# Graph attention followed by a graph convolution: p v by 26 products per 4-by-4 blocks of p instead of 28, with the block sums on GpSimd

## The chip, the cores and the metric

One core of a Trainium2 chip runs the whole program; the other cores are idle. The metric is device time in microseconds (us). Everything is in float32. The engines are called as in the profile: PE (TensorE, matmuls; PEld are its weight loads), DVE (VectorE), ACT (ScalarE), POOL (GpSimd) and SP (SyncE, which here only issues DMAs).

## The reference

```python
# x: 4096 x 512, adj: 4096 x 4096 (symmetric pattern, about 1 % of entries set)
q, k, v = x @ Wq.T + bq, x @ Wk.T + bk, x @ Wv.T + bv
a = q @ k.T / sqrt(512) + adj + adj
x = layernorm(x + softmax(a) @ v)
h = relu(adj @ (x @ W1) + b1)          # W1: 512 x 128
x = layernorm(x + adj @ (h @ W2) + b2)
```

Layer 0 has two large products, the scores q k^T and p v (p is the softmax's numerator). Layer 1 has two products with adj, of 128 columns each.

## The kernel before, in words

**Products of blocks.** Each large product is made of 2-by-2 blocks with seven block products in place of eight (Winograd's form). Sums of blocks of the left and of the right operand are made ahead on DVE and POOL or read from DRAM, and each product's PSUM result is added to the output quarters by DVE. ORDER (1, 2, 6, 7, 5, 4, 3) is the order of the seven; products 1, 6, 5, 3 collect in one PSUM bank and 2, 7, 4 in another, so that sums over products come from the accumulation in PSUM.

**Groups, units and gaps.** Scores and p are held transposed: keys on partitions, queries along columns. The 4096 queries are eight groups g of 512 columns. A group's scores take 16 units (two units for each 512 keys, d = 0 to 7), and a unit has seven gaps. In the main loop a gap does this in order: the hooks put there (`at`, `run`); a pair of score matmuls (`qk`, L423, 128x256, K of 256); if the pair is the second of its product, the read of its PSUM bank (`qk_read`, L436, one DVE add of 128x512 into S, where adj already lies); then the p reads that were due before the gap began; then items from a list `todo`, as many as a budget in us allows. A matmul item of p v counts 0.43. The schedule is by hand: each engine carries out its instructions in the order in which the program gives them out.

**What stands in the lists.** During group 0's scores the list holds the products for u = M x (`u_fast`, L243) and v = x Wv (`v_fast`, L342, one call for each 512 rows) for all rows, and the sums of v's blocks (`sum_v`, L371: four of 128x512 on POOL for each 512 rows; `store_v`, `store_sums`). During the scores of group g + 1 it holds group g's p v, from unit 2 on, and around it the rows of the group before (`row_items`, L663: division by the sum, residual, layer norm, `add_b2`, and the projection by W1, `project` and `project2`). The last group's p v has no scores beside it. Then come the products with adj (L979, `strassen`) and the output rows.

**From scores to p.** `new_max` (L445, DVE, 128x512) keeps a running maximum; when the group is done it is turned and spread; `shift` (L469, DVE, 128x512) subtracts it, and `exps` (L473, ACT, 128x1024) takes the exponential in place, two key tiles at a time. PREP says in which unit and gap each is done.

**p v before.** `px_items` (L536) goes through the 16 pairs of key tiles in five blocks of 2, 2, 4, 4, 4 pairs (BLOCKS). In each block it takes the seven products in ORDER; one product has two row halves r and accumulates over the block's pairs, one matmul (L553, 128x257 or 128x256, K of 128) for each pair and half: 16 x 7 x 2 = 224 matmuls a group, 1792 in all. The 257th column is a column of ones beside v, which gives the softmax's denominator. The left operand's sums are made in place in S, pair by pair: `px_t2` (L494, L495) on POOL, `px_t34` (L501) and `px_t1` (L506) on DVE in between the products. The right operands, blocks of v and their sums, are loaded by SP, one DMA of 256 or 512 KB for each product of a block (`load_x`, L485), three ahead. `px_read` (L524) adds a PSUM result to the output tile OT, 560 reads in all.

**What else lies in the way of these.** `add_b2` (L638) makes x1 + b2 on POOL (L641) in a tile `xb` of the ring of eight `sa` tiles (the pool `sap`), and POOL issues its store (L643); SP fills the other places of that ring with score operands (`load_s`, L307 and L312). The pool `adjp` has 12 slots of 1 MB for S, for v's tiles and, later, for chunks of adj, given out by the framework's pool in turn. The PSUM tag "o" has four banks, also in turn; x and y hold the scores.

Of the kernel before, what the change touches and what calls it, by code (L numbers as in the profile page):

```python
# [20 lines left out]
CW = 1024  # L21


@with_exitstack
def tile_graph_attention_then_gcn(
# [87 lines left out]
    BLOCKS = ((0, 2), (2, 4), (4, 8), (8, 12), (12, 16))  # L113
    vs_d = {a: dram.tile([P, 7, b - a, HW], F32, name=f"vs_d{a}") for a, b in BLOCKS}
# [11 lines left out]
    xnp = att.enter_context(tc.tile_pool(name="xnp", bufs=2, side="right"))  # L126
    form = ExitStack()
    mp = form.enter_context(tc.tile_pool(name="mp", bufs=1, side="right"))
    m_t = mp.tile([P, ND, D], F32, name="m_t")
    g_t = mp.tile([P, D], F32, name="g_t")  # L130
    ms_t = mp.tile([P, 2, 2, HW], F32, name="ms_t")
    xtp = form.enter_context(tc.tile_pool(name="xtp", bufs=2, side="right"))
    uop = form.enter_context(tc.tile_pool(name="uop", bufs=1, side="right"))

    def bank(tag, name, bufs=1):
        return psum.tile([P, W], F32, tag=tag, name=name, bufs=bufs)
# [59 lines left out]
    def u_fast(b):  # L196
# [41 lines left out]
        def one(k, j):  # L238
            def go():
                if j == 0 and k in (1, 2, 7):  # L240
                    X["X" if k == 1 else "Y"] = bank("o", f"psu{b}_{k}", 4)
# [72 lines left out]
    def x_rows(q):  # L314

        w = xnp.tile([P, 2, D], F32, tag="xn", name=f"w{q}", padded_shape=[P, 2, D + 4])
        nc.sync.dma_start(w, x[ts(q, 2 * P), :].rearrange("(r p) d -> p r d", p=P))
        T["x_rows", q] = lambda r: row_parts(2 * q + r, w[:, r])

    def v_fast(d):  # L320
# [3 lines left out]
        def read(k):  # L324
            ps = X["X" if k in (1, 6, 5, 3) else "Y"].rearrange("p (j o) -> p j o", j=2)
            t, o = QUARTER[k]
            to = VW[d][:, 2 * t + o]
            if k in (1, 6, 7, 3):
                nc.scalar.copy(to, ps)
            else:  # L330
                nc.vector.tensor_tensor(to, ps, to, ALU.add)
            if k == 4:
                store_v(d)

        def one(k, j):
            def go():
                if (k, j) == (1, 0):
                    VW[d] = v_room(d)
                if j == 0 and k in (1, 2, 7):
                    X["X" if k == 1 else "Y"] = bank("o", f"psv{d}_{k}", 4)  # L340
# [21 lines left out]
    def v_place(d):  # L362
        a = max(a for a, _ in BLOCKS if a <= 2 * d)
        return vs_d[a][:, :, 2 * d - a : 2 * d - a + 2, :]

    def store_v(d):
        to = v_place(d)
        nc.scalar.dma_start(to[:, 0], VW[d][:, 0])
        nc.scalar.dma_start(to[:, 1:3], VW[d][:, 2:4])

    def sum_v(d):  # L371
        a11, a21, a12, a22 = (VW[d][:, k] for k in range(4))
        tt = nc.gpsimd.tensor_tensor
        tt(a22, a21, a22, ALU.add)
        tt(a21, a21, a11, ALU.subtract)
        tt(a11, a22, a11, ALU.subtract)
        tt(a12, a12, a11, ALU.subtract)

    def store_sums(d):
        nc.gpsimd.dma_start(v_place(d)[:, 3:7], VW[d])  # L380


    def begin_scores(g, d):

        S[g, d] = adjp.tile([P, 2, 2, W], F32, tag="adj", name=f"s{g}_{d}")
# [85 lines left out]
    def exps(g, q):  # L471
        ck = pair(g, q)
        nc.scalar.activation(ck, ck, AF.Exp, scale=2.0)  # L473

    PHASES = [(g, a, b, k) for g in range(NG) for a, b in BLOCKS for k in ORDER]

    def load_x(n):
        g, a, b, k = PHASES[n]
        if n < 4:
            pool = xnp2 if n % 4 > 1 else xnp  # L480
            XN[n] = pool.tile([P, 4, HW + 1], F32, tag="xn", name=f"xn{n}")
            nc.gpsimd.memset(XN[n][:, :, HW:], 1.0)
        XN[n] = XN[n % 4]
        place = {1: 0, 2: 1, 4: 2, 6: 3, 7: 4, 3: 5, 5: 6}[k]
        nc.sync.dma_start(XN[n][:, : b - a, :HW], vs_d[a][:, place])  # L485

    def quarters(g, q):
        ck = pair(g, q)
        return ck[:, 0, :HW], ck[:, 0, HW:], ck[:, 1, :HW], ck[:, 1, HW:]

    def px_t2(g, q):

        b11, b12, _, b22 = quarters(g, q)
        nc.gpsimd.tensor_tensor(b12, b12, b11, ALU.subtract)  # L494
        nc.gpsimd.tensor_tensor(b12, b22, b12, ALU.subtract)  # L495

    def px_t34(g, q):

        b = pair(g, q)[:, :, :HW]
        t2 = pair(g, q)[:, 0, HW:].unsqueeze(1).to_broadcast([P, 2, HW])  # L500
        nc.vector.tensor_tensor(b, b, t2, ALU.subtract)  # L501

    def px_t1(g, q):

        _, t2, _, b22 = quarters(g, q)
        nc.vector.tensor_tensor(t2, b22, t2, ALU.subtract)  # L506
# [3 lines left out]
    def px_read(g, first, k, r):  # L510

        letter = "PX" if k in (1, 6, 5, 3) else "PY"
        ps = T[letter, r][:, : HW + 1]
        f, i = QUARTER[k]
        to = OT[g][:, 2 * i + r, f]

        def go():
            if first and k in (1, 6, 7, 3):
                if g == NG - 1:
                    nc.vector.tensor_copy(to, ps)  # L520
                else:
                    nc.scalar.copy(to, ps)
            else:
                nc.vector.tensor_tensor(to, ps, to, ALU.add)  # L524

        px_reads.append((letter, go))

    def read_px(letters=("PX", "PY")):
        for one in list(px_reads):
            if one[0] in letters:  # L530
                px_reads.remove(one)
                one[1]()
# [3 lines left out]
    def px_items(g):  # L536
        def one(n, r, q):
            _, a, b, k = PHASES[n]

            def go():  # L540
                letter = "PX" if k in (1, 6, 5, 3) else "PY"
                if q == a:
                    if r == 0:
                        if n + 3 < len(PHASES):
                            load_x(n + 3)
                        if k in (6, 5, 3, 4, 7):
                            read_px((letter,))
                        if k == 1 and a == 0:
                            OT[g] = rowp.tile([P, PER, 2, HW + 1], F32, tag="ot", name=f"ot{g}", bufs=2)
                    if k in (1, 2):  # L550
                        T[letter, r] = bank("o", f"p{n}_{r}", 4)
                cols = HW + (k != 6)
                nc.tensor.matmul(  # L553
                    T[letter, r][:, :cols],
                    quarters(g, q)[{1: 0, 2: 2, 6: 1, 7: 0, 5: 1, 4: 2, 3: 3}[k]][:, ts(r, P)],
                    XN[n][:, q - a, :cols],
                    start=k in (1, 2, 7) and q == a,
                    stop=q == b - 1,
                    skip_group_check=True,
                )  # L560
                if r == 1:
                    if k == 6:
                        px_t34(g, q)
                    if k == 7:
                        px_t1(g, q)
                if q == b - 1:
                    px_read(g, a == 0, k, r)
# [4 lines left out]
            one(n, *((m % 2, a + m // 2) if k in (6, 7) else (m // (b - a), a + m % (b - a))))  # L572
            for n, (g_, a, b, k) in enumerate(PHASES)
            if g_ == g
            for m in range(2 * (b - a))
# [87 lines left out]
    def row_items(g, between):  # L663
# [6 lines left out]
        def pro(r):  # L670
            return [item(0.44, project, g, r)]

        def pro2(r):
            return [item(0.9, project2, g, r)]
# [15 lines left out]
    with tc.tile_pool(name="wqk", bufs=1) as wp:  # L690
# [53 lines left out]
        for o in range(ND):  # L744
            turned(wq_t, wq_n, o, bank("o", f"psq{o}", 4))
# [5 lines left out]
        psm = [bank("o", f"psm{a}", 4) for a in range(ND)]  # L751
# [30 lines left out]
    SLOTS = 12  # L782

    adjp = ctx.enter_context(tc.tile_pool(name="adjp", bufs=SLOTS))
    v_ring = [adjp.tile([P, 4, 2, HW], F32, tag="adj", name=f"vw{n}") for n in range(3)]
    wv_t = adjp.tile([P, 2, 2, 2, HW], F32, tag="adj", name="wv_t")
    v_ring.append(t_sb[:, :16].rearrange("p (k j a) b -> p k j (a b)", k=4, j=2))

    def v_room(d):
        return v_ring[(0, 1, 2, 0, 1, 3, 2, 3)[d]]  # L790

    wv_t4 = accp.tile([P, 2, HW], F32, tag="lacc", name="wv_t4")
# [36 lines left out]
    for d in range(NG):  # L829
        if d:  # L830
            first += [(0.86, f) for f in u_fast(d)]
        late = [(0.86, f) for f in v_fast(d)]
        if d:
            late[4:4] = [(0, lambda d=d: sum_v(d - 1))]
            late[12:12] = [(0, lambda d=d: store_sums(d - 1))]
        first += late
    first += [
        (0.86, lambda: owing.pop()()), (0.86, lambda: sum_v(NG - 1)), (0, lambda: store_sums(NG - 1))
    ]
# [75 lines left out]
    def load_to(u):  # L915

        while len(CK) < min(2 * u + 2, len(loads)):
            j, tiles, i, cols = loads[len(CK)]
            ck = adjp.tile([P, tiles, cols], F32, tag="adj", name=f"ck{len(CK)}")
# [14 lines left out]

    def b_side(u):
# [7 lines left out]
        def t13(m):  # L943
            TT[m] = adjp.tile([P, 3, W], F32, tag="adj", name=f"tt{m}")
# [13 lines left out]
    def open_block(n):  # L958
        w = blocks[n][2]
        BK[n] = {  # L960
            k: bank(BANKS[k], f"b{n}_{k}", 4 if BANKS[k] == "o" else 1)[:, :w] for k in (1, 2)
        }

    def product(u, k):

        n, q0, pairs = UNITS[u]
        if k not in BK[n]:
            w = blocks[n][2]
            BK[n][k] = bank(BANKS[k], f"b{n}_{k}", 4 if BANKS[k] == "o" else 1)[:, :w]
# [17 lines left out]
    def strassen(n, beside, done=()):  # L987
# [51 lines left out]
    EARLY, MID, LATE = (1, 2, 4), (2, 4, 6), (3, 5, 6)  # L1039
    PREP = [  # L1040
        (1, (2, 3, 4)), (1, (4, 5, 6)), (2, LATE), (3, MID), (4, EARLY), (4, LATE), (5, EARLY), (5, LATE),
# [271 lines left out]
```

## Time and profile before

| | |
|---|---|
| median of three runs | 2307.99 us (2307.57 to 2308.24) |
| the profiled execution | 2308.46 us, of which the profile's span is 2306.7 |
| mean granted TensorE clock | 0.996 |
| instructions in the span | 28379 |
| group 1's first add_b2 tile to group 2's (L641) | 778.58 to 981.51 us |
| DMA traffic | 528 MB, 229 GB/s over the span; 203 to 207 GB/s in mid-kernel, 331 in the stretch from 1900 us |

Times in a profile line are us; in a group's line the columns are the form and count, then busy time and mean ns of one, then the idle time of the engine just before and what ended most of it. A PE record is a half of a matmul: one float32 matmul of the program leaves two MATMUL records and two weight loads, so the 1792 matmuls of p v are x3584 at L553. In a timeline line the columns are start, duration, engine, line, operation and form, and in brackets how long the engine was idle before and what ended it. In a line of windows the columns are the window, its length, then busy time and count for PE, PEld, DVE, ACT and POOL, the granted clock, the share of the DMA engines' time, and GB/s.

### The profile page before, as it was taken

To read this page: it belongs to the slowest core of one execution; us is meant where nothing else is said; L and a number is where in the kernel's file an instruction comes from. 1 tells how busy PE (TensorE), PEld (TensorE's weight loads), DVE (VectorE), ACT (ScalarE), POOL (GpSimd) and SP (SyncE) were. 2 spreads that over 40 slices of the span, in tenths; PEclk is the share of its full clock that TensorE was granted. 3 is DMA by queue.
4 is the path that set the end of the run, shared out by engine and by line. 5 is a ranking of instruction groups with operands and counts; after the bars stand their busy time and mean duration, and the time that the engine had idled before them with its cause. 6 is when DMAs were issued, how large, how long until landed. Compare 5 with 4: busy or idle time off the path is not lost.

```text
span 2306.7 us, 28379 instructions
## 1 busy us (share of the span) xinstructions
PE 2270.1 (98%) x10732; PEld 1769.0 (77%) x10732; DVE 1475.5 (64%) x2526; ACT 287.9 (12%) x409; POOL 534.2 (23%) x651
## 2 busy tenths in 40 slices
PE   9999999999999999999999999999998999999998
PEld 6888888888888888888888888888886743333455
DVE  5454556656656665665666567566656877888864
ACT  2111111002101100210120021002002100000012
POOL 2242341112211311231131123113113720101143
PEclk9999999999999999999999999999999999999999
DMA  5656676574665667466666756666546568999996
GB/s 184 210 214 213 220 265 217 184 258 160 219 223 190 211 192 251 157 216 222 200 191 203 254 164 210 218 211 196 193 155 219 173 250 329 333 349 375 356 377 196
DMA packets 324791, 528.27 MB, mean 229 GB/s; under 512 B 18416, under 2 KB 190960, under 8 KB 323504
## 3 DMA queue, kind: packets, MB, share of 16 engines
q1 hardware_dynamic: 272128, 404.81, 52.7%
q10 hardware_dynamic: 43408, 85.21, 10.5%
q0 software_dynamic: 9120, 36.44, 4.1%
q8 instruction: 86, 1.41, 0.2%
q14 instruction: 49, 0.40, 0.0%
HBM read 472.13 MB, written 52.69 MB: 228 GB/s over the span
## 4 chain that ended last, share of the span: by engine, by line
PE 89%; issue 5%; DVE 4%; POOL 1%; DMA 0%; ACT 0%; POOLq 0%; DVEq 0%; ACTq 0%
PE p L553 29%; PE X L423 18%; PE b L979 14%; PE Y L423 13%; PE psv L342 4%; PE psu L243 4%; PE acce L1258 2%; PE tps L658 1%; PE ops L1212 1%; DVE s L501 1%; PE x1ps L649 1%; DVE stats L623 1%; PE psm L754 1%; DVE s L469 0%; DVE s L436 0%
## 5 line engine op out<-in xcount | busy, mean ns | idle before, releaser
L553 PE MATMUL p<-xn,s 128*128 128x257 f32 (+1 forms) x3584 | 913.7, 381 | 14.4 <-DVE s L501 9.4
L553 PEld LDWEIGHTS p<-xn,s 128*128 128x128 f32 x3584 | 678.8, 191 | 120.0 <-DVE s L501 13.2
L423 PE MATMUL X<-ut,sa 128*128 128x256 f32 x1984 | 513.6, 381 | 3.8 <-DVE s L436 3.8
L423 PEld LDWEIGHTS X<-ut,sa 128*128 128x128 f32 x1984 | 369.3, 189 | 68.8 <-DVE s L436 20.3
L436 DVE TENSOR_TENSOR s<-X,s 128x512 f32<-128x512 f32 x256 | 176.8, 690 | 322.4 <-PE X L423 321.8
L423 PE MATMUL Y<-ut,sa 128*128 128x256 f32 x1408 | 360.6, 379 | 0.0
L494 POOL TENSOR_TENSOR s<-s 128x256 f32<-128x256 f32 x128 | 102.6, 802 | 881.1 <-ACT s L473 879.9
L436 DVE TENSOR_TENSOR s<-Y,s 128x512 f32<-128x512 f32 x192 | 132.6, 691 | 265.9 <-PE Y L423 265.7
L423 PEld LDWEIGHTS Y<-ut,sa 128*128 128x128 f32 x1408 | 265.7, 189 | 37.1 <-DVE s L436 0.2
L473 ACT ACTIVATE s<-s 128x1024 f32<-128x1024 f32 x128 | 135.3, 1057 | 833.9 <-DVE s L469 829.9
L524 DVE TENSOR_TENSOR ot<-p,ot 128x257 f32<-128x257 f32 x496 | 202.3, 418 | 36.7 <-PE p L553 36.1
L469 DVE TENSOR_TENSOR s<-s,mb 128x512 f32<-128x512 f32 x256 | 189.3, 741 | 7.4 <-ACT mb L399 7.4
L445 DVE TENSOR_TENSOR macc<-macc,s 128x512 f32<-128x512 f32 x240 | 183.7, 765 | 0.3
L946 DVE TENSOR_TENSOR tt<-ck 128x1024 f32<-128x1024 f32 x112 | 139.3, 1280 | 36.2 <-PE b L979 31.5
L979 PE MATMUL b<-tt,st 128*64 128x512 f32 (+1 forms) x768 | 159.1, 545 | 3.1 <-DVE tt L950 3.1
L979 PEld LDWEIGHTS b<-tt,st 128*64 128x64 f32 x768 | 55.1, 138 | 93.5 <-issue 79.5
L495 POOL TENSOR_TENSOR s<-s 128x256 f32<-128x256 f32 x128 | 105.8, 827 | 10.0
L979 PE MATMUL b<-ck,t_sb 128*64 128x512 f32 x384 | 96.7, 595 | 0.0
L501 DVE TENSOR_TENSOR s<-s 128x512 f32<-128x512 f32 x128 | 93.7, 746 | 0.0
L950 DVE TENSOR_TENSOR tt<-ck,tt 128x512 f32<-128x512 f32 x112 | 81.7, 765 | 0.0
L581 POOL TENSOR_TENSOR xr<-xr,bv_t 128x512 f32<-128x512 f32 x32 | 43.6, 1394 | 136.9 <-DMA xr<-in_x_dram 119.9
L954 DVE TENSOR_TENSOR ck<-ck,tt 128x512 f32<-128x512 f32 x112 | 73.7, 693 | 0.0
(175 smaller groups left out, 1750.2 us busy)
## 6 DMA issues: line engine op xcount, KB each, us to landing
ck<-in_adjT_dram SPq DMA_DIRECT2D x128, 1024.0 KB, 7.5
xn<-vs_d SPq DMA_DIRECT2D x168, 512.0 KB, 4.3
s<-in_adjT_dram ACTq DMA_DIRECT2D x64, 1024.0 KB, 7.1
sa<-s_d SPq DMA_DIRECT2D x224, 256.0 KB, 4.4
sa<-in_xT_dram SPq DMA_DIRECT2D x168, 256.0 KB, 4.7
xn<-vs_d SPq DMA_DIRECT2D x112, 256.0 KB, 2.9
ut<-u_d SPq DMA_DIRECT2D x49, 256.0 KB, 6.9
xt<-in_xT_dram SPq DMA_DIRECT2D x8, 1024.0 KB, 9.2
```

The costliest lines, as they stand in the source:

```text
L423: nc.tensor.matmul(T["X" if k in (1, 6, 5, 3) else "Y"][:, ts(j, HW)], SA[g, d, a][:, c, j, :], UT[g, b][:, c, :], start=k in (1, 2, 7) an ...
L436: nc.vector.tensor_tensor(ck, ps, ck, ALU.add)
L445: nc.vector.tensor_tensor(MACC[g], MACC[g], ck[:, h, :], ALU.max)
L469: nc.vector.tensor_tensor(ck, ck, MB[g], ALU.subtract)
L473: nc.scalar.activation(ck, ck, AF.Exp, scale=2.0)
L494: nc.gpsimd.tensor_tensor(b12, b12, b11, ALU.subtract)
L495: nc.gpsimd.tensor_tensor(b12, b22, b12, ALU.subtract)
L501: nc.vector.tensor_tensor(b, b, t2, ALU.subtract)
L524: nc.vector.tensor_tensor(to, ps, to, ALU.add)
L553: nc.tensor.matmul(T[letter, r][:, :cols], quarters(g, q)[{1: 0, 2: 2, 6: 1, 7: 0, 5: 1, 4: 2, 3: 3}[k]][:, ts(r, P)], XN[n][:, q - a, :cols],
L946: nc.vector.tensor_tensor(t[:, :2], v[:, :, 1], v[:, 0], ALU.subtract)
L979: nc.tensor.matmul(BK[n][k][ts(half, HH)], lhs, right(u, i, half, b), start=q == 0, stop=q == NP - 1,)
```

## The change

p v now takes blocks of four pairs of key tiles (1024 rows, four blocks b for each group). p's block is seen as 4 by 4 parts of 128 queries by 256 keys, v's as 4 by 2 parts of 256 keys by 256 columns, and 26 products replace the 28 that the two-level form had. PRODUCTS lists them: bank, whether the bank begins anew, left part, place of the right operand, which kind of 257th column it has, and the outputs (row, half, sign, with or without column 257) that the bank is read into when the product is done. One product is two matmuls (c, the two 128-row halves of K), 52 for each block, 208 a group, 1664 in all. The four "o" banks are bound to the products' first entry.

- P_SUMS: 27 sums of parts of p for each block, [128, 2 x 128], in place in S with one spare tile `p_room`. Its first entry is the product at whose start the sum is given out. All on POOL, in the last group some (m % 5 in (1, 3)) on DVE. They replace `px_t2`, `px_t34` and `px_t1`.
- V_SUMS: 18 sums of parts of v for each 512 rows, 16 on POOL and the two marked "n" on DVE, in place of four of twice the size; they are given out in three sets, at items 3, 7 and 11 of the next 512 rows' v products. The stores are on POOL's queue; v's tiles have two rooms in place of four.
- 27 reads of PSUM for each block, 864 in all; an output's first read is on ACT, the others on DVE.
- `load_x` loads one operand of 256 KB for each product, 832 in all, four products ahead, into nine rooms of three kinds.
- The ring of 12 slots is one tile, given out by `slot()`. The exponentials are earlier (PREP): a block needs all of its four pairs at its first product. `begin_scores` is earlier by some gaps for two tiles of group 1. `project` and `project2` count 0 in the budget, and two spare products of the next stage stand later in the last group's list.

```diff
+V_SUMS = (
+    (1, 0, "+"), (3, 2, "+"), (0, 4, "-"), (1, 10, "n"), (5, 11, "+"), (3, 5, "-"), (2, 13, "+"), (4, 14, "-"),
+    (0, 6, "-"), (1, 16, "+"), (13, 16, "-"), (18, 15, "+"), (17, 7, "-"), (7, 3, "-"), (2, 21, "-"), (6, 22, "-"),
+    (10, 21, "+"), (12, 24, "n"),
+)
+P_SUMS = (
+    (1, 4, 4, 6, "+"), (1, 0, 0, 4, "-"), (2, 14, 13, 14, "+"), (2, 12, 12, 15, "+"), (2, 12, 14, 12, "+"),
+    (2, 4, 4, 12, "-"), (3, 16, 14, 0, "+"), (5, 14, 6, 14, "-"), (6, 16, 3, 4, "+"), (8, 0, 2, 0, "+"),
...
+    (16, 3, 12, 1, "-"), (18, 1, 1, 13, "-"), (18, 9, 1, 9, "-"), (19, 6, 12, 6, "-"), (20, 11, 8, 11, "+"),
+    (20, 16, 16, 11, "-"), (21, 3, 2, 3, "-"),
+)
+PRODUCTS = (
+    (0, 1, 0, 1, 0, ((0, 1, 1, 0),)), (1, 1, 13, 19, 0, ((3, 0, -1, 0),)),
+    (2, 1, 1, 2, 1, ((0, 0, 1, 1),)), (0, 0, 0, 11, 0, ((0, 0, -1, 0),)),
+    (3, 1, 4, 17, 2, ((2, 1, 1, 0), (3, 1, -1, 0))), (0, 0, 16, 10, 0, ((3, 0, -1, 0),)),
+    (3, 0, 12, 8, 1, ((3, 0, 1, 1),)), (0, 0, 14, 24, 0, ((1, 0, -1, 0),)),
+    (3, 0, 16, 6, 1, ((1, 0, 1, 1),)), (0, 0, 6, 12, 0, ((1, 1, 1, 0),)),
+    (3, 0, 0, 4, 1, ((0, 0, 1, 1),)), (0, 0, 12, 25, 0, ((3, 1, 1, 0),)),
...
+    (2, 0, 3, 14, 1, ((0, 1, -1, 0),)), (0, 0, 4, 20, 0, ((3, 1, 1, 0),)),
+    (2, 0, 9, 13, 0, ((2, 1, -1, 0),)), (3, 0, 6, 9, 1, ((2, 1, 1, 0),)),
+    (0, 0, 16, 7, 0, ((2, 1, -1, 0),)), (3, 0, 3, 5, 0, ((0, 1, 1, 0),)),
+    (2, 0, 10, 15, 0, ()), (2, 0, 11, 6, 1, ((2, 0, 1, 1),)),
+)
...
+    def sum_v(d, a, b):
+        to = vs_d[d // 2][:, :, d % 2]
+        if a == 8:
+            for lo, hi in ((1, 3), (4, 8)):
+                nc.gpsimd.dma_start(to[:, lo:hi], VW[d][:, lo:hi])
+        for n in range(a, b):
+            x, y, sign = V_SUMS[n - 8]
+            out_, x, y = v_operand(d, n), v_operand(d, x), v_operand(d, y)
+            if sign == "n":
+                nc.vector.scalar_tensor_tensor(out_, x, -1.0, y, ALU.mult, ALU.subtract)
+            else:
+                nc.gpsimd.tensor_tensor(out_, x, y, ALU.add if sign == "+" else ALU.subtract)
+        nc.gpsimd.dma_start(to[:, a:b], v_rooms[(a - 8) // 8 % 2][:, : b - a])
...
+    def px_read(g, b, k):
+        where, _, _, _, _, outs = PRODUCTS[k]
...
+        def go(ps, to, sign, first):
+            if first:
+                nc.scalar.activation(to, ps, AF.Copy, scale=float(sign))
+            elif sign > 0:
+                nc.vector.tensor_tensor(to, ps, to, ALU.add)
             else:
-                nc.vector.tensor_tensor(to, ps, to, ALU.add)
-
-        px_reads.append((letter, go))
+                nc.vector.tensor_tensor(to, to, ps, ALU.subtract)
+
+        for i, f, sign, last in outs:
+            first = b == 0 and (g, i, f) not in OT
+            OT[g, i, f] = True
+            cols = HW + last
+            args = T["p", where][:, :cols], OT[g][:, i, f, :cols], sign, first
+            px_reads.append((where, lambda args=args: go(*args)))
...
     def px_items(g):
-        def one(n, r, q):
-            _, a, b, k = PHASES[n]
+        def one(b, k, c):
+            n = g * PER_G + b * len(PRODUCTS) + k
+            where, begins, a, _, kind, _ = PRODUCTS[k]
 
             def go():
...
+                if c == 0:
+                    load_x(n + AHEAD)
+                    read_px(where)
...
+                    for m, (e, out_, x, y, sign) in enumerate(P_SUMS):
+                        if e == k:
+                            out_, x, y = (p_block(g, b, z) for z in (out_, x, y))
+                            eng = nc.vector if g == NG - 1 and m % 5 in (1, 3) else nc.gpsimd
+                            eng.tensor_tensor(out_, x, y, ALU.add if sign == "+" else ALU.subtract)
+                    if begins:
+                        T["p", where] = bank(f"o{where}", f"p{n}")
+                cols = HW + (kind > 0)
                 nc.tensor.matmul(
-                    T[letter, r][:, :cols],
-                    quarters(g, q)[{1: 0, 2: 2, 6: 1, 7: 0, 5: 1, 4: 2, 3: 3}[k]][:, ts(r, P)],
-                    XN[n][:, q - a, :cols],
+                    T["p", where][:, :cols],
+                    p_block(g, b, a)[:, c],
+                    XN[n][:, c, :cols],
...
+                if c == 1:
+                    px_read(g, b, k)
...
         def pro(r):
-            return [item(0.44, project, g, r)]
+            return [item(0, project, g, r)]
 
         def pro2(r):
-            return [item(0.9, project2, g, r)]
+            return [item(0, project2, g, r)]
...
+            for place, ab in ((11, (24, NV)), (7, (16, 24)), (3, (8, 16))):
+                parts[1][place:place] = [(0, lambda d=d, ab=ab: sum_v(d - 1, *ab))]
...
+    PREP = [(1, (2 + (q > 1), 2 + q, 2 + q)) for q in range(4)]
+    PREP += [(q - 2, MID) for q in range(4, NP)]
```

The main loop of gaps (qk, qk_read, the reads due, the items while more than 0.2 us of budget is owed) is as before.

## The prediction

> **What bounds the kernel now.** I read the page's first and fourth parts, then its groups, then the stages, then single waits.
>
> ```profile
> PE 2270.1 (98%) x10732; PEld 1769.0 (77%) x10732; DVE 1475.5 (64%) x2526; ACT 287.9 (12%) x409; POOL 534.2 (23%) x651
> PE 89%; issue 5%; DVE 4%; POOL 1%; DMA 0%; ACT 0%; POOLq 0%; DVEq 0%; ACTq 0%
> L553 PE MATMUL p<-xn,s 128*128 128x257 f32 (+1 forms) x3584 | 913.7, 381 | 14.4 <-DVE s L501 9.4
> L494 POOL TENSOR_TENSOR s<-s 128x256 f32<-128x256 f32 x128 | 102.6, 802 | 881.1 <-ACT s L473 879.9
> ```
>
> PE is busy 98% of the span and is 89% of the chain: time goes only with matmuls, or comes as PE waits. L553 waits 14.4 us in all. POOL has 881 us of slack before L494, but an average says nothing of what must be ready at a given matmul. By stages (PE first, granted clock third from the end):
>
> ```profile
> 545.00:770.00 225.00, 224.01 (x1071) 195.25 (x1071) 140.41 (x261) 33.01 (x46) 46.71 (x59) 1.00 0.62 203
> 1670.00:1900.00 230.00, 218.75 (x989) 161.38 (x987) 163.28 (x279) 27.94 (x32) 80.17 (x82) 0.98 0.59 197
> ```
>
> Mid-kernel PE is full; the last group's p v, alone, loses 11 us of 230. The timeline in mid-kernel gives my unit prices:
>
> ```profile
> 806.77 1.03 PE L423 MATMUL X<-ut,sa 128*128 128x256 f32 x4
> 807.63 1.03 PE L553 MATMUL p<-xn,s 128*128 128x256 f32 x4
> 807.83 0.69 DVE L436 TENSOR_TENSOR s<-X,s 128x512 f32<-128x512 f32 x1 [1.45 <-PE X L423]
> ...
> 808.58 0.73 PEld L423 LDWEIGHTS X<-ut,sa 128*128 128x128 f32 x4 [0.32 <-DVE s L436]
> ```
>
> Blocks start 0.86 apart (0.866 over many): two matmuls of four records, **0.433 us a matmul**. The score read starts 0.20 after the next block (1.06 after its own began: 0.20 after that block's end), lasts 0.69, and PE goes on 0.06 after its end (808.52 to 808.58). So a PE-to-DVE step costs 0.20, a DVE-to-PE step 0.06.
>
> **Part 1, fewer matmuls.** 1792 products' matmuls become 1664: 128 x 0.433 = **-55.4 us**, 6.9 a group, all on PE's path. L501 and L506 vanish, and with them PE's waits on them (5.3 in mid-kernel by the table of waits over 545 to 1670, about 1 before and beside it): **-6.3**; their waits in the last group are in part 5.
>
> **Part 2, reads stand behind the score read (the main loss).** Reads grow from 560 to 864. In total DVE hardly changes: per group it loses 16 L501 (11.7) and 16 L506 (7.0) and gains some 100 reads of 0.42 for 62 before. What counts is the place. A product is now two matmuls, and its PSUM bank is wanted again two products later in most of the list. A read is emitted in the gap after its product, behind that gap's score read if the gap has one (every second gap). The 208 p items of a group over 112 gaps give 0.80 us per gap, so most gaps hold two items and 16 hold one. After a one-item gap the pairs of a product straddle two gaps until the next one. There the built order is: score pair, one p matmul, then the matmul that reuses the bank; on DVE: score read (waits for the pair), then the p read that the matmul needs. From the pair's end: 0.20 + 0.69 + 0.03 (DVE's step) + 0.42 (L524) + 0.06 = 1.40, covered by one matmul of 0.433: **PE waits 0.97**. I count such places in the built order: products 5, 7, 9 and 20 of each 1024-row block (in the first block 9's read is on ACT): 15 a group, 14.6 us; product 22 of the last block has both matmuls behind it and waits 1.76; a fuller DVE at the turn of the group adds 0.5. 16.8 a group, seven groups with scores beside: **+118**. Ends: 0.88 each with the shortest rows (93 in all), 1.3 if an L445 or L469 (0.74, 0.77) is sometimes ahead on DVE (150). Nearest row for size: L501's waits of PE, 9.4 us in 8, mean 1.2. The same counting on the kernel before finds 0.09 per score tile and about one cluster of L501 waits per group, as its trace has. Nothing hides these: PE has one queue, and everything behind waits too.
>
> **Part 3, the chain of block sums on POOL.** 27 sums a block at about 0.80 (L494) on POOL: 4 x 27 x 0.80 = 87 us of a group's 200, so on average POOL fits. But the four add_b2 tiles of a group come from the same ring slot, and each waits on POOL until the one before has been stored:
>
> ```profile
> 1191.32 0.56 POOL L643 DMA_DIRECT2D x_d<-xb  x1 [0.30 <-POOL xb L641]
> 1197.13 1.27 POOL L641 TENSOR_TENSOR xb<-xr,b_t 128x512 f32<-128x512 f32 x1 [5.25 <-DMA x_d<-xb]
> 1198.69 0.56 POOL L643 DMA_DIRECT2D x_d<-xb  x1 [0.30 <-POOL xb L641]
> 1205.28 1.26 POOL L641 TENSOR_TENSOR xb<-xr,b_t 128x512 f32<-128x512 f32 x1 [6.03 <-DMA x_d<-xb]
> ```
>
> 1.27 + 0.30 + 0.56 and 5 to 6 idle: 8 us a tile. Before, the sums behind had a unit to spare. Now the order on POOL is: last sum of block 0, tiles 0 to 2, two sums of block 1, tile 3, five sums. Tile 3 starts about 16 us after product 21 began, takes 2.1, and four sums bring 21.2; product 4 of block 1 wants the fourth, nine products (9 x 1.8 = 16.2 us) after product 21. PE waits 5 (1.6 to 6.7 with landings of 2.3 to 6.8); I take 4.5 x 6 groups = **+27** (10 to 40). SP's sa load that takes the tiles' slot waits as well (57.3 us in the waits of SP before), but the x loads up to product 9 stand ahead of it: nothing, or 2 a group if a landing is slow.
>
> **Part 4, the sums of v in the first stage.** 18 sums per 512 rows for 4; 16 of 128x256 on POOL (0.80) with DMA issues of 0.57: some 16 us. They are given out over eight items of 1.3 = 10.4 us, and the last is on DVE and needs POOL's. DVE stands 5.6 us, a score read behind it comes late, and the next 512 rows' first score pair, which takes the same bank, waits about 3.2. Six times = 19; at the end two sets run back to back with u's sums, and group 1's first scores wait 5 to 10: **+28** (15 to 42).
>
> **Part 5, the last group.** No scores stand beside p v; a product takes 0.87 and its bank is back after 1.73, while DVE holds 42 reads, 19 sums, the shifts and the rows, some 87 of 102 us. Against the 11 us lost now I take 20: **+10** (0 to 20).
>
> **Part 6, at nothing.** Single loads: 256 KB per 1.8 us product adds 100 MB; by the windows 203 GB/s becomes some 265, against 331 in the tail. They are given out four products (7.2 us) ahead and land in 2.9 (page, part 6). If that cover went, 0.1 a product would be 83 us. Earlier exps, the ring by hand, the memset, the budget of 0 for the projections: the order moves, no work; +-5.
>
> **The clock.** Waits in clusters lower it:
>
> ```profile
> 1743.51 4.32 PE L553 MATMUL p<-xn,s 128*128 128x257 f32 x10 [1.22 <-DVE s L501]
> ```
>
> Ten records take 2.16 at the usual pace; here, after waits of 1.60, 0.22 and 1.22, they took 4.32, so 2.2 were lost; single waits of 1.92 and 1.63 elsewhere left the clock at 1.00. Part 2's waits stand 4.5 us apart, thinner than that cluster; part 3's, of some 4.5, are longer than it. I take nothing for the first and some 2 us for each of the six others: **+10** (0, if none falls; 40, if one in six of part 2's waits also costs 2).
>
> The Trainium skill ("TensorE: Matmul & The Clock Gate", Part 1: The HAM clock gate) puts the fall after an idle window of about 3.4 us. The row shows a fall with no gap that long. By the page alone the sum would hold the same +10, by the row at its worst +40.
>
> A rule of the skill speaks against the change: "SBUF — State Buffer" says that a DVE instruction with two SBUF inputs and a GpSimd instruction lock each other out of a shared port pair. L494 takes 0.72 at the least, 1.02 beside an L469, so the trace agrees. By the rule at its worst every sum takes 1.02 and POOL is late by 0.2 x 4 sums, 0.9 more in each wait of part 3.
>
> **Sum**, against the profiled execution's 2308.46 (span 2306.7 and 1.8 around it): -55.4 - 6.3 + 118 + 27 + 28 + 10 + 10 = +131, 2440. The median of the runs is 0.5 lower, which changes nothing: **2440**. Ends: all low 2308.5 - 61.7 + 93 + 10 + 15 = 2365; all high 2308.5 - 61.7 + 150 + 40 + 42 + 20 + 40 = 2539.
>
> **Rivals.**
> 1. Faster: DVE's reads hide. If bank reuse were covered (a second matmul beside each place, 1.40 against 0.87 plus PE's own lag), part 2 falls to under 20; with parts 3 and 4 at their low ends the time is 2308.5 - 61.7 + 20 + 25 = 2292. It decides once the loss per place is under about 0.3 us. For it: DVE is busy 64%. Against it: both steps, 0.20 and 0.06, and both durations are measured, and the order is built. Chance 0.07; same within 0.2% on its edge, 0.02.
> 2. Only the chains on POOL cost: parts 3, 4, 5 without half of part 2: 2380. For it: PE may run late at these places for another reason and find the read done. Chance 0.14.
> 3. Heavier: DVE busy at most places, POOL slowed by the ports, the clock down at each cluster of three waits: 2500 and over. For it: the window 1740 to 1760 fell to 0.83. Chance 0.12.
> 4. It does not do what it says: the loads, not PE, set the pace of p v. DMA is at 0.63 of its engines' time mid-kernel and would be at some 0.80; 0.1 to 0.3 late a product is +83 to +250. Chance 0.04.
> The forecast itself, 2395 to 2490, 0.61.
>
> The range, 2365 to 2520, holds the forecast, the second rival and the near half of the third. A step of 0.2% is about what a measurement of this kernel can tell. Faster 0.07, same 0.02, slower 0.91.
>
> **What would show it.** The group period, 202.6 now by the first add_b2 tiles (778.58 to 981.51), becomes about 214; L553's successor waits some 110 to 130 us on DVE's p reads, about 1.0 each, and 25 to 30 on POOL sums in waits near 4.5, early in the second block; X L423 waits about 3.2 on its score read in each part of the first stage. If p's waits on DVE are under 40 us in all, part 2 is wrong; if the waits name loads of v, part 6 is.

## The result, and the profile after

| | before | after |
|---|---|---|
| median | 2307.91 us (2307.57 to 2308.24, 4 runs) | 2479.47 us (2475.96 to 2486.84, 4 runs) |
| profiled execution | 2308.46 | 2486.84, 7 above the median |
| span | 2306.7 | 2485.1 |

The ratio is 1.0748, with a 95% interval of 1.0723 to 1.0772: the change makes the kernel 172 us slower. The page of the kernel after, its first and fourth parts and the groups that answer to those shown of before:

```profile
PE 2285.8 (92%) x10476; PEld 1751.2 (70%) x10476; DVE 1482.2 (60%) x2634; ACT 292.7 (12%) x417; POOL 1035.7 (42%) x1343
...
PE 66%; POOL 13%; issue 10%; DVE 6%; DMA 5%; SPq 0%; ACT 0%; POOLq 0%; ACTq 0%; DVEq 0%
...
L582 PE MATMUL p<-vo,ring 128*128 128x256 f32 (+1 forms) x2944 | 802.6, 388 | 108.3 <-POOL ring L578 41.3
L578 POOL TENSOR_TENSOR ring<-ring 128x256 f32<-128x256 f32 x732 | 570.3, 791 | 675.9 <-PE p L582 515.3
...
L461 PE MATMUL X<-ut,sa 128*128 128x256 f32 x1984 | 520.6, 386 | 12.6 <-DVE ring L474 10.3
```

PE has 256 fewer records and is busy 15.7 us longer: a matmul of p v is no slower in itself, but some run at a lowered clock. PE's share of the span falls from 98% to 92% and of the chain from 89% to 66%. No other engine is full: POOL has doubled to 42%, DVE is at 60%. So it is waits. The table of waits of PE (us in total, times, longest):

```profile
PE p L582 <- POOL ring L578: 41.3, 26, 4.7
PE X L461 <- DVE ring L474: 41.2, 9, 8.2
PE p L582 <- issue: 35.3, 52, 3.0
PE p L582 <- DVE ot L544: 26.6, 29, 6.9
PE p L582 <- POOL rstd L649: 9.3, 6, 1.6
PE p L582 <- DMA vo<-vs_d: 6.7, 3, 3.8
...
PE p L582 <- DVE ot L542: 3.6, 4, 1.7
```

The lines of p L582 on POOL ring, on issue and on DVE ot mix two things, as the experiments show: many waits of 0.7 us whose releaser the profile guesses differently each time, and few long ones. The six on POOL rstd are of one kind: 1.55 us, each at the same product of a group's first block. Where the time came from is better read by stages. The marks are the ACT copy that spreads a group's maximum (L399 before, L437 after) and the last add_b2 tile:

| us of the profiled execution | before | after | difference |
|---|---|---|---|
| start to group 0's maximum (first stage) | 326.9 | 386.2 | +59.4 |
| from there to group 7's maximum (seven groups) | 1401.5 | 1486.5 | +85.0 |
| the last group, to its last add_b2 tile | 147.0 | 176.5 | +29.5 |
| the rest | 431.3 | 435.8 | +4.5 |

In mid-kernel the waits look like this (timeline of the kernel after):

```profile
1325.03 1.03 PE L461 MATMUL X<-ut,sa 128*128 128x256 f32 x4
...
1326.09 0.69 DVE L474 TENSOR_TENSOR ring<-X,ring 128x512 f32<-128x512 f32 x1 [2.23 <-PE X L461]
1326.70 0.41 DVE L544 TENSOR_TENSOR ot<-ot,p 128x256 f32<-128x256 f32 x1
...
1327.16 0.70 PE L582 MATMUL p<-vo,ring 128*128 128x256 f32 x2 [0.68 <-DVE ot L544]
```

The score pair ends at 1325.89 (0.866 after its start); one p matmul follows to 1326.32; the next needs a bank whose read stands behind the score read and starts at 1327.16. That is 0.84 late, and the first records after a wait take another 0.1: 0.95 lost. A group has 13 to 15 such waits.

### The profile page after: what moved, and what is told of

Same layout as the page of the kernel before. It is cut to its first block, busy times and chain, and to the rows that moved or that the text cites. A ratio compares the mean times of both kernels' runs of the same rounds, so it can differ in the third digit from the quotient of the medians.

```text
span 2485.1 us, 29881 instructions
## 1 busy us (share of the span) xinstructions
PE 2285.8 (92%) x10476; PEld 1751.2 (70%) x10476; DVE 1482.2 (60%) x2634; ACT 292.7 (12%) x417; POOL 1035.7 (42%) x1343
## 4 chain that ended last, share of the span: by engine, by line
PE 66%; POOL 13%; issue 10%; DVE 6%; DMA 5%; SPq 0%; ACT 0%; POOLq 0%; ACTq 0%; DVEq 0%
PE p L582 24%; PE X L461 14%; PE b L1024 12%; PE Y L461 9%; POOL ring L578 3%; POOL t_sb L418 2%; POOL ring L418 2%; DMA ring<-in_adjT_dram 2%; DVE ring L474 1%; DMA vo<-vs_d 1%; PE acce L1303 1%; DMA x_d<-xb 1%; POOL uo L264 1%; POOL xb L663 1%; PE psu L285 1%
## 5 line engine op out<-in xcount | busy, mean ns | idle before, releaser
L582 PE MATMUL p<-vo,ring 128*128 128x256 f32 (+1 forms) x2944 | 802.6, 388 | 108.3 <-POOL ring L578 41.3
L578 POOL TENSOR_TENSOR ring<-ring 128x256 f32<-128x256 f32 x732 | 570.3, 791 | 675.9 <-PE p L582 515.3
L582 PEld LDWEIGHTS p<-vo,ring 128*128 128x128 f32 x2944 | 554.2, 193 | 226.3 <-POOL ring L578 72.0
L461 PEld LDWEIGHTS X<-ut,sa 128*128 128x128 f32 x1984 | 374.2, 192 | 81.4 <-DVE ring L474 29.4
L474 DVE TENSOR_TENSOR ring<-X,ring 128x512 f32<-128x512 f32 x256 | 176.5, 689 | 409.4 <-PE X L461 365.7
L511 ACT ACTIVATE ring<-ring 128x1024 f32<-128x1024 f32 x128 | 135.1, 1057 | 911.9 <-DVE ring L507 833.9
L1024 PE MATMUL b<-ring,st 128*64 128x512 f32 (+1 forms) x1024 | 223.7, 543 | 3.5 <-DVE ring L995 3.5
L542 DVE TENSOR_TENSOR ot<-p,ot 128x256 f32<-128x256 f32 (+1 forms) x472 | 193.5, 418 | 36.1 <-PE p L582 32.5
L507 DVE TENSOR_TENSOR ring<-ring,mb 128x512 f32<-128x512 f32 x256 | 191.4, 759 | 10.6 <-ACT mb L437 10.6
L483 DVE TENSOR_TENSOR macc<-macc,ring 128x512 f32<-128x512 f32 x240 | 182.5, 760 | 0.2
L991 DVE TENSOR_TENSOR ring<-ring 128x1024 f32<-128x1024 f32 x112 | 140.5, 1266 | 53.7 <-DMA ring<-in_adjT_dram 46.9
L582 PE MATMUL p<-vo,p_room 128*128 128x256 f32 (+1 forms) x384 | 118.3, 396 | 26.9 <-issue 14.2
L582 PEld LDWEIGHTS p<-vo,p_room 128*128 128x128 f32 x384 | 71.8, 195 | 50.7 <-issue 24.6
```

The costliest lines, as they stand in the source:

```text
L461: nc.tensor.matmul(T["X" if k in (1, 6, 5, 3) else "Y"][:, ts(j, HW)], SA[g, d, a][:, c, j, :], UT[g, b][:, c, :], start=k in (1, 2, 7) an ...
L474: nc.vector.tensor_tensor(ck, ps, ck, ALU.add)
L483: nc.vector.tensor_tensor(MACC[g], MACC[g], ck[:, h, :], ALU.max)
L507: nc.vector.tensor_tensor(ck, ck, MB[g], ALU.subtract)
L578: eng.tensor_tensor(out_, x, y, ALU.add if sign == "+" else ALU.subtract)
L582: nc.tensor.matmul(T["p", where][:, :cols], p_block(g, b, a)[:, c], XN[n][:, c, :cols], start=begins == 1 and c == 0, stop=c == 1, skip_gr ...
```

## The experiments

Theory: three separate losses, each a thing that stands in a queue ahead of what PE needs: the p reads behind the score read on DVE (part 2 of the prediction), the add_b2 chain ahead of the block sums on POOL (part 3), and DVE's "n" sums of v ahead of the score read (part 4). Rivals: POOL has too much to do, whatever the order; or one resource lies behind all three.

**Reads first.** One edit in the main loop:

```diff
             if g < NG:
                 qk(g, d, k, j)
-                if j == 1:
-                    qk_read(g, d, k)
             for _ in range(ready):
                 px_reads.pop(0)[1]()
+            if g < NG and j == 1:
+                qk_read(g, d, k)
```

> Only the order on DVE changes: in each gap the p reads that are due go out ahead of the score read instead of behind it. Theory: PE's 14 to 15 short waits a group (0.7 us idle, 0.95 lost each) are for a p read that stands behind the score read, so they go: 13 us a group, seven groups, 2479 becomes about 2390, and the group period 215 becomes about 202. Rival (the block sums on POOL, which the table of waits names for 41 us, hold p v up): the short waits stay, 2470 to 2480.

Measured: 2394.21 us (2388.24 to 2398.46), ratio to the kernel before 1.0374 (1.0354 to 1.0395): 85 us less than the kernel after. The same stretch of time in the kernel after and in this run (PE's busy time first, clock third from the end):

```profile
1000.00:1200.00 200.00, 186.38 (x857) 157.65 (x856) 117.78 (x226) 25.52 (x33) 87.59 (x117) 0.98 0.75 243
```

```profile
1000.00:1200.00 200.00, 196.02 (x916) 169.09 (x915) 129.20 (x241) 24.98 (x33) 102.15 (x128) 0.99 0.82 270
```

In 200 us PE gets 916 records done in place of 857, while POOL works more in the same time, not less: 102 us for 88. The block sums were not what held p v up; many of the "POOL ring" and "issue" waits were for the p read. The group period falls from about 215 to between 199 and 204.

**The same edit in the kernel before.**

> The kernel before with the one edit of the run in which the due p reads go out ahead of the score read. Theory: the order alone costs nothing; it costs only where a PSUM bank is wanted again after one matmul, and the kernel before gives its banks back two products of four to eight matmuls later. So 2308, within 3 us. Rival (DVE's order costs PE time in any such kernel, the change only shows it more): 20 us or more faster than 2308.

Measured: 2306.08 us (2303.51 to 2307.64, 10 runs), ratio 0.9992 (0.9983 to 1.0001). The order on DVE is worth 1.5 us there, next to nothing. By the program a bank is wanted again there mostly after four matmuls of p v and more, in the kernel after mostly after two. That the shorter distance is what turned a harmless order into a loss is argued from this; the two runs show that the order costs something only with the change.

**add_b2 in place.**

```diff
-        xb = sap.tile([P, D], F32, tag="sa", name=f"xb{g}_{r}")
-        nc.gpsimd.tensor_tensor(xb, XR[g][:, r, :], b2_t, ALU.add)
+        xr = XR[g][:, r, :]
+        xb = xr if g < NG - 1 else sap.tile([P, D], F32, tag="sa", name=f"xb{g}_{r}")
+        nc.gpsimd.tensor_tensor(xb, xr, b2_t, ALU.add)
```

> Groups 0 to 6 make x1 + b2 in place in the row tile instead of in a tile of the score operands' ring, so that no add_b2 waits on POOL for the store of the one before. Theory: the one wait of 4.1 to 4.7 us a group at product 4 of the second block goes, six times, 2479 becomes about 2452; nothing else moves. Rival (POOL is late there because 27 sums a block are too many for it, with or without the stores): the wait stays above 3 us and the time within 5 us of 2479.

Measured: 2457.49 us (2451.52 to 2461.62), ratio 1.0642 (1.0622 to 1.0662): 22 less. This is what went, POOL in the kernel after at the second block of group 4's p v (the tiles are those of group 3's rows), with PE's wait (the first fence from POOL's timeline, the second from PE's):

```profile
1301.62 1.26 POOL L663 TENSOR_TENSOR xb<-xr,b_t 128x512 f32<-128x512 f32 x1 [4.86 <-DMA x_d<-xb]
...
1309.05 1.27 POOL L663 TENSOR_TENSOR xb<-xr,b_t 128x512 f32<-128x512 f32 x1 [3.73 <-DMA x_d<-xb]
```

```profile
1314.60 0.70 PE L582 MATMUL p<-vo,ring 128*128 128x257 f32 x2 [4.11 <-POOL ring L578]
```

POOL sits idle for two stores while PE's sums stand behind. The six waits of this kind are 3.72, 3.17, 4.34, 4.11, 2.26 and 2.98, 20.6 in all. With the tiles in place no POOL wait on a store of these is left in groups 0 to 6, and of PE's six waits one is left, of 1.70.

**The sums of v spread out.**

```diff
-            for place, ab in ((11, (24, NV)), (7, (16, 24)), (3, (8, 16))):
-                parts[1][place:place] = [(0, lambda d=d, ab=ab: sum_v(d - 1, *ab))]
+            f0, a0, a1, a2 = (0, 4, 2, 10) if d < NG - 1 else (1, 3, 7, 11)
+            for part, place, ab in ((1, a2, (24, NV)), (1, a1, (16, 24)), (f0, a0, (8, 16))):
+                parts[part][place:place] = [(0, lambda d=d, ab=ab: sum_v(d - 1, *ab))]
```

> The three sets of sums of v are given out over a whole 512 rows' time (in the next u products, then early and late in the v products) instead of over eight items of the v products; the same instructions. Theory: DVE no longer stands in front of the last sum of a set waiting for POOL, so PE's six waits of 5.0 to 5.5 us on the score read go, and with each the slow matmuls after it, 2.8 us: 6 x 8 = 48, 2479 becomes about 2432. If the clock does not matter, 31 are gained, 2448. Rival (POOL's whole work is too much for the first stage): the waits move to the stage's end, and under 15 us are gained.

Measured: 2427.08 us (2420.39 to 2433.93), ratio 1.0519 (1.0494 to 1.0544): 52 less. The kernel after at one of the six places:

```profile
103.11 0.73 POOL L418 TENSOR_TENSOR ring<-ring,t_sb 128x256 f32<-128x256 f32 x1
103.87 0.43 DVE L416 SCALAR_TENSOR_TENSOR ring<-ring 128x256 f32<-128x256 f32 x1 [6.44 <-POOL ring L418]
104.21 0.68 DVE L474 TENSOR_TENSOR ring<-X,ring 128x512 f32<-128x512 f32 x1
...
104.95 2.07 PE L461 MATMUL X<-ut,xt 128*128 128x256 f32 x4 [5.34 <-DVE ring L474]
...
106.82 3.62 PE L285 MATMUL psu<-xt,m_t 128*128 128x256 f32 x8
```

DVE stands 6.44 us for POOL's sum with a score read behind it, PE waits 5.34 for that read, and then four records take 2.07 and eight 3.62 in place of 1.03 and 1.89: the clock is down. The windows of the kernel after and of this run show both losses and that they are gone:

```profile
100.00:200.00 100.00, 85.03 (x356) 72.61 (x357) 40.56 (x69) 12.48 (x27) 50.32 (x60) 0.90 0.64 221
```

```profile
100.00:200.00 100.00, 100.00 (x465) 88.02 (x464) 53.12 (x87) 16.01 (x35) 65.42 (x77) 1.00 0.72 256
```

465 records in 100 us is what the kernel before has there too:

```profile
100.00:200.00 100.00, 100.00 (x465) 88.01 (x465) 50.55 (x81) 16.50 (x35) 34.40 (x31) 1.00 0.61 215
```

POOL does the same work in its slack.

**The three together.**

> The three edits together. Theory: they are separate losses and add up, 90 + 27 + 48 = 165 less, about 2315; what is left over the kernel before less 62 (2246) is then in the last group (30) and at the end of the first stage and the tail. Rival (one resource behind all three, so that each edit alone uncovers the next wait): 2370 to 2400.

Measured: 2326.45 us (2325.27 to 2328.71), ratio 1.0084 (1.0069 to 1.0099). 85 + 22 + 52 = 159 apart, 153 together: separate losses, not one resource. The seven groups now take 1372.1 us, 29.4 less than before; the first stage is still 13.4 above, the last group 28.3.

**What is left, 1: the end of the first stage.** On top of the three, the last sums of v of the last two sets are given out later, the very last by a hook in group 1's first unit.

```diff
+            for place, f in (
+                (14, lambda: sum_v(NG - 1, 16, 24)), (7, lambda: sum_v(NG - 1, 8, 16)),
+                (3, lambda: sum_v(NG - 2, 24, NV)),
+            ):
+                parts[1][place:place] = [(0, f)]
+            at(NP, 4, sum_v, NG - 1, 24, NV)
```

> On top of the three edits together (2326): the last sums of v of the last two sets of 512 rows are given out later (the very last ones after the stage), so that DVE does not stand before POOL's chain when group 1's scores begin. Theory: the waits of 8.15 and 2.2 us there and the slow matmuls behind them (3.2 and 1.8) mostly go, 2326 becomes about 2316. Rival (POOL's two sets back to back hold up something else as well, u's sums or the first block of p v): less than 4 us gained.

Measured: 2318.68 us (2314.05 to 2324.4), ratio 1.0049 (1.0034 to 1.0063): 8 less. The wait of 8.15 became 4.60, and one of 2.49 came new where PE spreads the maximum, so the theory (the waits there mostly go, 10 gained) held only in part.

**What is left, 2: the last group.** On top of the three:

```diff
+    def between_blocks(b):
+        if b < 2:
+            sum_t(0, 0, 8, (2 * b, 2 * b + 1))
+        elif b == 2:
+            sum_t(8, 8, 14)
+        else:
+            add_bv(NG - 1)
...
+                    if g == NG - 1 and k == 22:
+                        between_blocks(b)
...
-    at(last_unit - 5, 0, lambda: [sum_t(0, 0, 8), sum_t(8, 8, 14)])
```

> On top of the three edits together (2326): in the last group the work of other stages on POOL (sums of the projected rows, 8 instructions of 1 to 2 us; the addition of bv, 5.1 us in a row) is given out between two blocks, where no block sum is due. Theory: the waits of 4.7 and 6.9 us and the slow matmuls behind them (2.9 and 1.5) go, new ones of 2 or 3 come, 2326 becomes about 2314. Rival (DVE sets the last group's pace, so PE waits for its reads instead): under 5 us gained.

Measured: 2314.01 us (2310.91 to 2319.18), ratio 1.0034 (1.0021 to 1.0047): 12 less. The run of the three had these two waits, which the profile names by DVE's read and a block sum:

```profile
1823.97 3.79 PE L582 MATMUL p<-vo,ring 128*128 128x256 f32 x8 [4.72 <-POOL ring L578]
...
1855.87 1.22 PE L582 MATMUL p<-vo,ring 128*128 128x256 f32 x2 [6.90 <-DVE ot L544]
```

and POOL's and DVE's timeline of the same run tells what was under the second:

```profile
1847.61 5.10 POOL L603 TENSOR_TENSOR xr<-xr,bv_t 128x512 f32<-128x512 f32 x4
...
1852.67 2.26 POOL L578 TENSOR_TENSOR ring<-ring 128x256 f32<-128x256 f32 x3
1853.42 0.93 DVE L578 TENSOR_TENSOR ring<-ring 128x256 f32<-128x256 f32 x1 [5.16 <-POOL ring L578]
```

Adding bv to four rows stood in front of three block sums; DVE's own block sum waited for those, and its reads behind that. Afterwards both waits are gone, with one of 2.8 and one of 2.0 in their places.

**All of it.** Besides, adj's first chunks are loaded one at a time (`load_chunks`), sums 0, 2, 3 and 4 of a block are given out at product 24 of the block before, and group 6's rows begin 36 items later.

> All of these edits, and three more in the last group and at block starts: the loads of adj one at a time instead of four (PE waited 3.7 and 2.5 us there on loads of v that lay behind them), four of a block's sums that nothing must precede given out in the block before, and the rows of group 6 later, away from the shifts of group 7. Theory: 10 (stage end) + 12 (POOL) + 8 (loads, with the clock) + 5 (rows and sums), 2326 becomes about 2291, faster than the kernel before by some 0.7%. Rival (DVE-bound last group): 2305 to 2315.

Measured: 2292.82 us (2287.81 to 2296.06, 5 runs), ratio 0.9935 (0.9923 to 0.9948): 15 us faster than the kernel before, with the 26 products kept. First stage 334.6, seven groups 1362.4 (39 less than before), last group 160.0, rest 436.9. The mid-kernel window of this run, and the same of the kernel before:

```profile
1000.00:1200.00 200.00, 198.98 (x939) 172.05 (x938) 129.64 (x246) 25.53 (x33) 103.61 (x133) 1.00 0.83 276
```

```profile
1000.00:1200.00 200.00, 199.01 (x942) 173.07 (x941) 125.28 (x233) 25.13 (x33) 41.91 (x52) 1.00 0.63 204
```

PE is as full as before. The three added edits weren't tried one by one.

## Why the prediction was right or wrong

The time, 2479, is in the range (2365 to 2520) and the forecast's own stretch (2395 to 2490); the sum of 2440 was 39 too low, and its parts were not all right. That it came so near is in part luck: two parts were too high and the others, with the clock, too low.

- **Part 1 (-55.4 and -6.3): right.** A group of the last run takes 196.2 to 196.7 us against 202.6 (the stretch that the forecast gives for 202.6, 778.58 to 981.51, is 202.9; most others are 202.6), 6 less with a wait or two of about 1 us left in each.
- **Part 2 (+118): right in mechanism and place, 17 too large.** Counted off product by product in the trace, the short waits stand where the forecast put them: at products 5, 7, 9 and 20 of each block, 15 in group 0's p v and 13 to 15 in each of the six groups behind it (where product 5 of the second block is missing, part 3's wait stands just ahead of it). Each costs 0.95 (0.97 said). The one at product 5 of the first block idles 1.55 in groups 1 to 6 and costs 1.8. Together that is 101 in seven groups. The 1.76 for product 22 of the last block, 12 in all, is the term that failed: no wait shows there in these groups. Taking the order back gave 85 (89 by the profile's seven groups), since one to three of the short waits stay in a group. One of them, 0.96 at product 5 of the first block, is there in six groups with the reads first; the profile names POOL for it, and what holds it was not tried.
- **Part 3 (+27): right.** 20.6 of waits, mean 3.4 for the 4.5 taken, and 22 from the experiment. Product 4 of the second block, as said.
- **Part 4 (+28): the step that failed in size; 59 measured.** The mechanism and the six places were as said, but the wait was 5.0 to 5.5, not 3.2: POOL needed 18.9 us for the three sets (84.97 to 103.84), not 16. The sums took 13.5 of it (0.85 each, not 0.80), four store issues 3.4 (0.8 to 0.9 each, not 0.57), a store of u that lay between 0.6, and the rest was idle. And the clock, which I had set at nothing here, took 15.6 more. 30.9 of waits, 15.6 of slow matmuls, 8.2 and some 3 at the stage's end: 58 of the 59.
- **Part 5 (+10): failed.** 29.5 came, and the 6.9 that the fewer matmuls saved were eaten as well. I had counted DVE and overlooked that POOL also does other stages' work there: 12 us by the experiment. Four loads of 1 MB of adj also stand ahead of the loads of v on SP (in the run of the three at 1723.07), and PE waits 3.8 and 2.6 there for loads of v; the one edit against that was not tried alone. With every edit the last group still takes 13 more than before; what it would lose by DVE alone stays open.
- **Part 6 (nothing): right where it was argued,** mid-kernel, in the kernel after: of its three waits on loads of v, 6.7 us, only one of 0.3 lies ahead of the last group; wrong in the last group. And the cover is thin: the loads landed in 4.1 us (median), not 2.9, and in the faster runs, at 270 to 276 GB/s, PE does wait for loads of v mid-kernel by the profile's names, 4.0 in five with the reads first and 4.5 in five in the last run.
- **The clock (+10): too small.** By the spacing of PE's records over the usual 0.217, it cost some 21 in the first stage and at its end, and 5.6 in the six waits of part 3 up to the next wait (8 with the slow records behind that one). In the last group it cost 12 to 15 (before: 2.5 to 5), the higher figures with the first record after each wait.
- **The tail (+4.5)** wasn't foreseen; 3.5 of it are two waits on loads of adj that the kernel before does not have.

The errors in parts 2 and 3 (about 23 too much) hid a part of those in 4, 5 and the clock.

The signs that the forecast named did not all serve. The group period is 213 to 217 (214 said), and PE's waits on POOL at product 4 of the second block add up to 20.6 (25 to 30 said). But the waits of p on DVE are 30.2 by the table (26.6 and 3.6), under the 40 below which part 2 was to be wrong. The sign failed, not the part: the profile names the block sums or "issue" for most of these waits, and they went when the reads were put first.

Of the rivals, the second (POOL's chains alone) and the fourth (loads) are excluded by the runs with one edit each; the first too: the reads did not hide. The third (2500 and more) was nearer than I thought, by the clock, but through the long waits and not through part 2's.

## What to carry to other kernels

When a product gets shorter, look at every resource that was given back "a product later": the same order on the engine that frees it can turn from harmless (0.9992 when changed in the old kernel) into 85 us. On an engine that works in order, ask of each instruction that waits for another engine or a DMA what stands behind it and who needs that; an engine that is busy for 42% or 60% of the span can still hold PE up. And read a stall by taking one thing out: the profile's releaser was the block sum for waits that vanished when a read was moved.

## What the runs showed of the hardware

How far a wait of PE brings its clock down, in the kernel after, by what the next records lost up to the next wait: six waits of 5.0 to 5.5 us lost 2.4 to 2.8 each, always, one of 8.2 about 3, and those of 4.7 and 6.9 in the last group 2.7 and 2.3. Two of 4.1 and 4.3 lost 1.0 and 1.6. The single ones of 2.3, 3.0, 3.2 and 3.7 lost 0.1, 1.2, 0.1 and 1.6, and one of 2.2 at 393.61 lost 1.8. In the last group, where waits of 2.2 to 3.8 stand close together, they lost 1.8 to 2.8. Six single waits of 1.55, and the waits of 0.7, which often stand 4.4 us apart, lost no more than 0.1 each. The slow records start 0.427 us apart in place of 0.217. The Trainium skill ("TensorE: Matmul & The Clock Gate", Part 1: The HAM clock gate) gives an idle window of about 3.4 us, free-running. The sure loss from 4.7 us on and the mixed results below fit that, but single waits of 2.2 and 2.98 lost 1.8 and 1.2, so 3.4 us is no safe bound here.

The rule on the shared port pair ("SBUF — State Buffer", Who interferes with whom), cited in the forecast, shows no higher price than before: 732 block sums beside DVE's work took 791 ns on average, against 802 and 827 for the same form before. Single sums do take longer than the shortest, up to 1573 ns for 716, as the rule would have it. The sums were not compared with POOL alone, so no run here gives its price.
